# Pairing the leftover choices: a five-way branch near the end of a two-layer mixture kernel

## The chip, the cores and the metric

The kernel runs on one core of a Trainium2 chip. The metric is device time in microseconds (us) of that core, the median of several runs. A core has TensorE (PE in the profile; its weight loads are shown as PEld), VectorE (DVE), ScalarE (ACT), GpSimd (POOL) and SyncE (SP), each with an instruction stream of its own; the streams meet at semaphores.

## The reference, cut to what matters

Sixteen batches of 256 rows of 256 numbers pass through two residual layers. Layer 0 picks one expert of eight per batch (the largest entry of that batch's row of `cond_8`); layer 1 picks the two largest, weights them, and adds an expert that all batches share.

```python
# layer 0, per batch: expert = argmax(cond_8[b]); hidden size 512
out = (silu(x @ wu.T + bu) * (x @ wg.T + bg)) @ wd.T + bd
x = x + out
# layer 1, per batch: the two largest of softmax(cond_8[b]), weights w normed; hidden size 1024
out = sum(w[k] * ((gelu(x @ g[sel[k]]) * (x @ u[sel[k]])) @ d[sel[k]]) for k in range(2))
x = x + out + (gelu(x @ gs) * (x @ us)) @ ds       # the shared expert, for every batch
```

All is float32. Layer 1 thus has 32 routed choices (16 batches times two) and 16 shared ones. Which experts they fall on is known only when the kernel runs.

## The kernel before

**Units.** Work comes in units. A `Single` is one batch with one expert. A `Pair` is two batches that use the same expert; it multiplies both with Strassen's seven products in place of eight (`STEPS`), in Winograd's form. Its sums of weight blocks are made on POOL (`sums_a`, lines 353 to 357), those of x and of the hidden values on VectorE (`sums_b`, 346 to 349). A unit of layer 1 is cut into four quarters of the hidden size (two in layer 0). A single's quarter is 8 "up" matmuls (line 546, `p` and `pl`) and 4 "down" matmuls (line 575, `po`); a pair's is 14 up matmuls (line 407, banks X, Y, Q) and 7 down matmuls (line 458, `dX`, `dY`, `dQ`). All are 128 x 128 by 128 x 256.

**Order.** A routing computation on VectorE (`choices`, `order_of_work`) sorts the choices of each layer so that batches with the same expert stand side by side, and those without a partner at the end. 32 choices over 8 experts leave at most 8 experts with an odd number, so at least 12 pairs exist whatever the inputs: `NP2 = (NA - E) // 2` is 12. The last 8 positions (`NS2`) may or may not have partners. The kernel runs them all as singles. The sequence of units is fixed when the kernel is built:

```python
units = [*l0_pairs, *shared[:NF], *pairs, *ones[:-1], *shared[NF:]]
```

that is: 4 pairs of layer 0 with singles of layer 0 among them, 3 shared pairs, the 12 routed pairs, 7 singles, 5 shared pairs; the eighth single (`lone`) runs its quarters inside those of the fourth shared pair. Expert and batch numbers are read at run time from the sorted lists into registers of SP and POOL (`held`, line 235), so loads and stores have computed addresses.

**Timing by hand.** The instructions stand in the order that a hand-written clock gives (`Line`): `main` runs an up step and advances the clock, `later` puts a step some ticks behind (a pair's seventh up step, its activation, its downs), `flush` emits what is due. At each quarter `ahead` issues what later quarters need: `load_q` five quarters ahead (a 512 KB weight quarter, line 284, on SP's queue), the pair's POOL sums and `load_x` three ahead, `sums_x` one ahead, and `load_d` (1 MB, line 296) in the unit's own first quarter (its second in a layer 0 pair). Results go out on POOL's queue (`send`, line 329, an accumulating store in layer 1). The last pair adds to what stands in `out`, which `load_z` reads back in that pair's second quarter (j == 1), and stores from SP and ScalarE (line 494).

**Buffers** come from rotating pools with a number of buffers per tag (6 weight quarters `q`, 5 sums `s`, 2 down weights `d`, 3 results `ys` and so on), and PSUM banks X, Y, Q (two each), A and B (one each) likewise.

## Time and profile before

| what | value |
|---|---|
| runs | 1067.0, 1067.0, 1065.17 us (median 1067.0) |
| the profiled execution | 1065.7 us, of which the span from first to last instruction is 1064.1 us |
| matmul records on TensorE | 4858 (two for each fp32 matmul of the program) |
| granted TensorE clock | 1.00 |
| DMA | 146.26 MB, mean 137 GB/s |
| weight quarters loaded in layer 1 | 112 of 512 KB |
| ScalarE | 30% busy |

How to read the page: its first part gives each engine's busy time, share and number of instructions; the second cuts the span into 40 slices, each digit a busy share in tenths; the fourth follows the chain of work that ended last back from the end, so that shares in it are shares of what sets the time; a group row reads line, engine, operation, output<-input, shape, count, then busy time and mean ns, then idle time before it and what ended that. In a stretch's row the numbers after its length are the busy times of PE, PEld, DVE, ACT and POOL with instruction counts, then the granted clock, the DMA share and GB/s. A timeline row is start, length, then the instructions merged into it; a record of 1.89 us can overlap the next, as matmuls are pipelined.

### The profile page before, as it was taken

The numbers are of one execution on the slowest core, as the hardware profiler recorded it, in microseconds if no ns is written. First come the engines' busy times: TensorE is split into PE (matmuls) and PEld (weight loads), VectorE is DVE, ScalarE is ACT, GpSimd is POOL, SyncE is SP. The second block draws the span as 40 slices with busy tenths as digits, with TensorE's granted clock in tenths as the row PEclk, the third lists the DMA queues.
The fourth block names the chain that finished last, engine by engine and source line by source line (L and its number), as shares of the span: only waits on it lengthen the run. The fifth ranks groups of instructions, "written<-read, shape, count | busy, mean of one in ns | idle before, by whom it ended". The sixth has DMA issues, their size and how long they took to land.

```text
span 1064.1 us, 14030 instructions
## 1 busy us (share of the span) xinstructions
PE 1055.8 (99%) x4858; PEld 921.7 (87%) x4858; DVE 681.1 (64%) x1070; ACT 323.6 (30%) x516; POOL 472.7 (44%) x570
## 2 busy tenths in 40 slices
PE   9999999999999999999999999999999999999998
PEld 6788888888888888888888888888888888888887
DVE  7888775677767776777677777741111136767774
ACT  2222233333333333333333333321111122333331
POOL 2554454745663565466456535200000245554530
PEclk9999999999999999999999999999999999999999
DMA  7555565543453355235524542454656653453232
GB/s 254 188 198 195 182 206 169 177 131 91 117 139 99 99 133 140 88 96 139 139 99 100 139 129 85 114 148 127 171 198 178 183 183 119 129 139 102 61 76 40
DMA packets 50231, 146.26 MB, mean 137 GB/s; under 512 B 5234, under 2 KB 16114, under 8 KB 46578
## 3 DMA queue, kind: packets, MB, share of 16 engines
q1 hardware_dynamic: 35826, 124.66, 35.0%
q0 software_dynamic: 14048, 20.45, 11.2%
q8 instruction: 39, 0.64, 0.2%
q10 hardware_dynamic: 288, 0.26, 0.1%
q14 instruction: 30, 0.25, 0.1%
HBM read 124.38 MB, written 20.97 MB: 137 GB/s over the span
## 4 chain that ended last, share of the span: by engine, by line
PE 97%; DVE 1%; DMA 1%; issue 0%; SPq 0%; ACT 0%; DVEq 0%
PE X L407 21%; PE Y L407 14%; PE Q L407 14%; PE dX L458 11%; PE po L575 7%; PE p L546 7%; PE pl L546 7%; PE dQ L458 7%; PE dY L458 7%; DMA x<-x_dram 1%; PE spin L96 1%; DVE sq_z L159 0%; SPq L235 0%; ACT L433 0%; SPq L284 0%
## 5 line engine op out<-in xcount | busy, mean ns | idle before, releaser
L390 ACT ACTIVATE u<-X 128x512 f32<-128x512 f32 x264 | 157.6, 597 | 466.3 <-PE X L407 466.1
L354 POOL TENSOR_TENSOR s<-q 128x256 f32<-128x256 f32 x88 | 76.2, 865 | 252.5 <-PE Q L407 185.2
L407 PE MATMUL Y<-x,q 128*128 128x256 f32 x704 | 181.5, 380 | 2.4 <-DVE act L565 2.4
L407 PE MATMUL Q<-x,s 128*128 128x256 f32 x704 | 180.7, 379 | 0.0
L434 DVE TENSOR_TENSOR bt<-c 128x1024 f32<-128x1024 f32 x80 | 113.1, 1413 | 102.7 <-ACT c L433 102.7
L407 PE MATMUL X<-x,s 128*128 128x256 f32 x672 | 173.0, 380 | 0.0
L329 POOL DMA_DIRECT2D out_dram<-ys x46 | 47.5, 1032 | 255.3 <-ACT ys L587 108.5
L407 PEld LDWEIGHTS Y<-x,q 128*128 128x128 f32 x704 | 132.8, 190 | 22.8 <-DVE act L565 2.8
L407 PEld LDWEIGHTS Q<-x,s 128*128 128x128 f32 x704 | 133.8, 190 | 18.2
L407 PEld LDWEIGHTS X<-x,s 128*128 128x128 f32 x672 | 127.1, 190 | 19.1 <-issue 2.1
L394 DVE TENSOR_TENSOR c<-u,Q 128x512 f32<-128x512 f32 x176 | 119.8, 680 | 27.8 <-ACT u L390 23.4
L394 DVE TENSOR_TENSOR c<-u,Y 128x512 f32<-128x512 f32 x176 | 119.5, 679 | 11.7 <-PE Y L407 11.7
L557 DVE TENSOR_TENSOR act<-gel,pl 128x512 f32<-128x512 f32 x32 | 22.0, 686 | 124.7 <-PE pl L546 124.7
L575 PE MATMUL po<-act,d 128*128 128x256 f32 x384 | 89.8, 380 | 0.8 <-DVE act L565 0.7
L407 PE MATMUL X<-x,q 128*128 128x256 f32 x352 | 90.3, 379 | 0.0
L546 PE MATMUL pl<-x,q 128*128 128x256 f32 x368 | 86.9, 379 | 0.0
L546 PE MATMUL p<-x,q 128*128 128x256 f32 x368 | 86.9, 379 | 0.0
L433 ACT ACTIVATE c<-c 128x1024 f32<-128x1024 f32 x80 | 84.2, 1052 | 8.3 <-DVE c L394 7.6
L458 PE MATMUL dX<-bt,ds 128*128 128x256 f32 x352 | 83.9, 379 | 0.0
L458 PE MATMUL dQ<-bt,ds 128*128 128x256 f32 x352 | 83.8, 379 | 0.0
L458 PE MATMUL dY<-bt,d 128*128 128x256 f32 x352 | 83.8, 379 | 0.0
L575 PEld LDWEIGHTS po<-act,d 128*128 128x128 f32 x384 | 72.8, 190 | 11.4 <-DVE act L565 1.1
(117 smaller groups left out, 1324.2 us busy)
## 6 DMA issues: line engine op xcount, KB each, us to landing
q<-wq_dram SPq DMA_DIRECT2D x112, 512.0 KB, 3.5
d<-wd_dram SPq DMA_DIRECT2D x28, 1024.0 KB, 6.5
out_dram<-ys POOLq DMA_DIRECT2D x54, 256.0 KB, 4.4
x<-x1d SPq DMA_DIRECT2D x48, 256.0 KB, 4.1
q<-wq_dram SPq DMA_DIRECT2D x22, 514.0 KB, 4.0
d<-wd_dram SPq DMA_DIRECT2D x12, 513.0 KB, 5.4
x<-x_dram SPq DMA_DIRECT2D x15, 256.0 KB, 4.3
x1d<-ys POOLq DMA_DIRECT2D x8, 256.0 KB, 2.6
```

What stands on the lines that cost most here:

```text
L96: nc.tensor.matmul(spin, lhsT=idle[:, :P], rhs=idle, start=True, stop=True)
L329: nc.gpsimd.dma_start(row(out), ys[:, :, t, :], accum_op=ALU.add)
L354: tt(s("S1"), a("A21"), a("A22"), ALU.add)
L390: nc.scalar.activation(t, self.banks["X", j], AF.Copy)
L394: nc.vector.tensor_tensor(self.c[j][:, block].rearrange("p m s -> p (m s)"), self.copies[n, j], self.banks[tag, j], op,)
L407: nc.tensor.matmul(self.banks[tag, j][:, bass.ts(m, S)], lhsT=self.q[j][:, m, A_AT[a], :] if a in A_AT else self.s[j][:, m, S_AT[a], :], r ...
L433: nc.scalar.activation(u, u, AF.Gelu_apprx_tanh)
L434: nc.vector.tensor_tensor(t[:, 0:4, :], u, v, ALU.mult)
L458: nc.tensor.matmul(d, lhsT=src[:, j, :], rhs=self.acts[j][:, B_AT[b], :], start=OPENS[k] and j == 0, stop=j == self.kp - 1, skip_group_che ...
L546: nc.tensor.matmul(dst[:, bass.ts(half, S)], lhsT=self.q[j][:, m, 2 * half + c, :], rhs=self.xt[:, c, :], start=(c == 0), stop=(c == KD - 1),)
L557: nc.vector.tensor_tensor(act, gel, pu[1], ALU.mult)
L575: nc.tensor.matmul(self.po[:, bass.ts(c, S)], lhsT=self.d[:, 2 * c + half, j, :], rhs=self.acts[j][:, bass.ts(half, S)], start=(j == 0 and ...
```

## The change

Three things are changed.

1. **A count.** `order_of_work` for layer 1 already marks the last choice of each expert with an odd number (with 4096, in `count`). Now their sum is turned into `more`, the number of further pairs among the last 8 positions: 4 minus half the number of marks, as an integer `more_i` in SBUF.
2. **A branch.** All units up to the fifth shared pair and the first quarter lists of the sixth (`shared[-3]`) are emitted in common. Then every engine loads `more_i` into a register and jumps into one of five arms. Arm k runs the sixth shared pair, the 8 - 2k choices left as singles, k more pairs, and the last two shared pairs. Each arm is written out in full from the same saved state. There is no `lone` single any more. The weight load that would run five quarters ahead across the branch is the first load in the arm. `load_z` moves to the last pair's third quarter (j == 2). Three shared pairs run ahead of the 12 routed ones as before, but only two, not none, stand between these and the first single, besides the sixth in the arm.
3. **Fixed tiles.** The pools are replaced by lists of tiles of the same numbers and sizes (`RINGS`, `BANKS`), handed out in turn (`take`); for five tags a tile is returned by name (`give`), and steps that need one wait in the emission order until one is free (`when_free`).

The core of the diff:

```diff
+            yield red(more, count, AX.X, ALU.add)
+            nc.vector.tensor_scalar(more, more, -1.0 / (2 * 4096), NS2 / 2, ALU.mult, ALU.add)
+            yield nc.vector.tensor_scalar(more_i, more, 0.0, float(NS2 // 2), ALU.max, ALU.min)
...
+    def take(tag, *shape, of=None):
+
+        i = turns[tag].pop(0)
+        if tag not in HELD:
+            turns[tag].append(i)
+        else:
+            assert (tag, of) not in turns
+            turns[tag, of] = i
+        t = rings[tag][i]
...
+    def when_free(tag, f):
+
+        if turns[tag] and not turns["later", tag]:
+            f()
+        else:
+            turns["later", tag].append(f)
+
+    def give(tag, of):
+        turns[tag].append(turns.pop((tag, of)))
+        if turns["later", tag]:
+            turns["later", tag].pop(0)()
...
-            t = wp.tile([P, QB], F32, tag="q", name=f"q_{self.n}_{j}", bufs=6)
+            t = take("q", QB)
...
+    more_pairs = [Pair(next(names), 1, 2 * NP2 + 2 * i) for i in range(NS2 // 2)]
     ones = [Single(next(names), 1, 2 * NP2 + i) for i in range(NS2)]
-    lone = ones[-1]
-    units = [*l0_pairs, *shared[:NF], *pairs, *ones[:-1], *shared[NF:]]
-    units[-1].last = True
+    units = [*l0_pairs, *shared[:NF], *pairs, *shared[NF : NPR - NB]]
+    shared[-1].last = True
...
-            if u is units[-1] and j == 1:
+            if u is shared[-1] and j == 2:
                 u.load_z()
...
+    quarters += in_order(shared[-NB:-NB + 1])
+    run(units)
+    for _ in routing:
+        pass
...
+    common, entry = len(quarters), state()
+    which = nc.values_load(
+        more_i[0:1, 0:1],
+        min_val=0,
+        max_val=NS2 // 2,
+        skip_runtime_bounds_check_because="held between 0 and the largest when it is made",
+    )
+    for k in tc.Switch(which, NS2 // 2 + 1):
+        for o, d in entry:
+            o.clear()
+            o.update({n: v.copy() if isinstance(v, (list, dict)) else v for n, v in d.items()})
+        left = ones[2 * k :]
+        rest = [shared[-NB], *left, *more_pairs[:k], *shared[1 - NB :]]
+        quarters[common:] = in_order(rest)[shared[-NB].kp :]
+        u, j = quarters[common]
+        u.load_q(j)
+        run(rest)
+        line.flush(1 << 30)
+        line.send()
```

`NB` is 3 and `NS2` is 8.

## The prediction

> **What bounds the kernel now.** First the page's totals, the slices and the chain.

> ```profile
> span 1064.1 us, 14030 instructions
> ...
> PE 1055.8 (99%) x4858; PEld 921.7 (87%) x4858; DVE 681.1 (64%) x1070; ACT 323.6 (30%) x516; POOL 472.7 (44%) x570
> ...
> PE   9999999999999999999999999999999999999998
> ...
> PE 97%; DVE 1%; DMA 1%; issue 0%; SPq 0%; ACT 0%; DVEq 0%
> ```

> TensorE is busy in every slice and 97% of the chain is its own. So the time is the number of matmuls times the slot of one, plus the few places where TensorE stands still. The table by stretches for 330 to 696 us (pairs) and 696 to 878 us (mostly singles) says how few:

> ```profile
> 330.00:696.00 366.00, 365.96 (x1694) 320.64 (x1693) 267.23 (x388) 130.29 (x204) 188.07 (x206) 1.00 0.42 115
> 696.00:878.00 182.00, 182.00 (x845) 160.03 (x843) 39.72 (x60) 30.68 (x50) 27.87 (x31) 1.00 0.58 174
> ```

> The second column after the stretch is TensorE: no idle time in either, although VectorE (fifth number) works 73% of the pair stretch and 22% of the other. Asking for the waits of TensorE from 200 us to 1060 us gives none. A pair is therefore not held up by its extra sums, and a single not by its loads. The slot comes from the chain in order of time, in the stage of singles:

> ```profile
> 756.32 1.73 PE po L575 x8
> 758.05 1.73 PE p L546 x8
> 759.78 1.73 PE pl L546 x8
> ...
> 777.04 1.73 PE po L575 x8
> ```

> Each row holds 8 records, that is 4 matmuls of the program (an fp32 matmul leaves two records: 2,429 in the program, 4,858 on the page). Four quarters, one whole single, take 777.04 - 756.32 = 20.72 us for 48 matmuls: 0.4317 us each. A layer 1 pair has 84 matmuls (4 quarters of 7 x 2 up, 7 x 4 down), so 36.26 us; in the pair stretch the chain's piece "dX" at 237.34 recurs at 273.60 and 309.86, 36.26 us apart.

> **How far TensorE's sequencer runs ahead** decides what a branch costs. The built program has a semaphore wait of TensorE just ahead of each pair's first X matmul; the view of line 407 between 548.80 and 548.95 shows one, the timeline the matmuls after it:

> ```profile
> L407 PEldq EVENT_SEMAPHORE  x1: 51/51/51, 548.9 to 548.9; - x1
> ```

> ```profile
> 551.00 1.89 PE L458 MATMUL dY<-bt,d 128*128 128x256 f32 x8
> 552.73 1.03 PE L407 MATMUL X<-x,q 128*128 128x256 f32 x4
> ```

> The wait was over at 548.9 us, the matmul behind it began at 552.73: at the end of a pair the sequencer stands 3.8 us ahead of the array, and the same number recurs at each pair's end. The new branch is put in exactly such a place (Y, then four dY matmuls, then the next pair's X).

> [...]

> ```profile
> q8 instruction: 39, 0.64, 0.2%
> ```

> 39 packets of 16 KB[...]. [...]

> **The change, part by part.**

> *Which arm runs.* The two largest of each row of cond_8 as drawn by the reference choose experts 0 to 7 for 6, 2, 6, 3, 4, 4, 2, 5 batches. Halved and rounded down: 15 pairs, two choices left. Twelve are sure, so three more are paired: the fourth arm runs (three pairs, two singles).

> *Matmuls.* Three pairs replace six singles: 3 x (2 x 48 - 84) = 36 fewer of 2,429 (the built program agrees: 1,759 before the branch and 634 in that arm). 36 x 0.4317 = **15.5 us off the path**.

> *Loads.* Six singles load 24 q and 6 d, three pairs 12 and 3: 15 SP loads less, 9.4 MB. Nothing waited for them, so no gain.

> *Sums added.* 60 POOL operations at 0.865 us (the row of line 354), some 52 us, and about 21 us of VectorE per pair (26.5 for a pair, 267.2/366.0 of 36.26, less eight products of 0.686 from the row of line 557). Hidden: the 330 to 696 us stretch carries just this density of pairs with 0.04 us of TensorE idle. POOL sums start three quarters (27 us of pairs, 15 us of singles) ahead and need 3.5 us. If that cover went, TensorE would stand for the missing part of 3.5 us at each of 12 quarters.

> *Fixed tiles.* In the built program every engine's instructions keep their order up to the stage of singles, apart from three tiny VectorE operations for the count; TensorE has slightly fewer waits, POOL more (each some 20 to 50 ns while POOL idles 56%). The tile orders name the same readers. Cost 0. The z load is issued one quarter later and a store, its POOL queue and SP wait for it; z has more than 20 us until the last pair's downs. Cost 0.

> *The branch.* On each of five engines: a register load, two register steps, an indirect branch, the fetch of the arm's first block. The first register load of SP took 466 ns, of POOL 492 ns:

> ```profile
> L235 SPq TENSOR_LOAD <-bs x64: 262/272/517, 13.7 to 1010.1; - x64
> ```

> Take 0.5 us, 0.4 us for moves and branch, and for the fetch 2.4 us: 0.9 us for a 16 KB packet (0.2% of 16 x 1064 us over 39) and 1.5 us of latency, an estimate from the 128 KB stores that land in 1.8 us. Sum 3.3 us; bounds 2 and 7 us, as no row shows such a fetch.
> On **TensorE** this starts 3.8 us ahead of the array: 0 exposed at 3.3 us, 3.2 us at 7. **ScalarE** reaches its branch when the last pair's third X step ends, six matmuls (2.6 us) before TensorE's branch point, and must copy the first new X two matmuls (0.9 us) after it; TensorE's wait for that copy ends 0.9 us ahead of need in an earlier pair (by line 407's view the wait began at 552.9 and took 1512 ns, the X matmul behind it started at 555.32). Cover 2.6 + 0.9 + 0.9, some 4.2 us with the latency of a semaphore. Behind it in its queue stand the copies that free X; TensorE waits for them. **VectorE** ends its last sums 2 us after the branch point, and the first result that TensorE needs (a Y bank used again) is due 8 us after. **POOL and SP** reach the branch 16 and 20 us before TensorE (waits on earlier matmuls), and then wait anyway. So a fetch is covered on every engine up to a total of about 3.8 us; I take 0.7 us for refilling the queue and a fetch somewhat over cover, from 0 to 5 us. Not below zero: a branch saves no work.

> *Sum.* Against the profiled execution, 1065.7 us (span 1064.1 and 1.6 around it): 1065.7 - 15.5 + 0.7 = 1050.9. The median of the runs, 1067.0, lies 1.3 above it and gives 1052.2. I take **1051.5 us**. A difference of 0.2% (2.1 us) is what can be told from none.

> **Rivals.**
> 1. *The branch is exposed*: fetch 5 to 10 us, five engines fetching at once beside 16 busy queues[...]. For: no cold fetch is in the trace. Against: packets of 0.9 us. 2 to 7 us back: 1053.5 to 1058.5.
> 2. *Slower*: after the jump the streaming doesn't resume, and every block of the arm is fetched cold on TensorE. The arm holds 634 x 4 instructions and its waits, ten blocks; from 1.55 us exposed per block the gain is gone, at 3 us the time is 1065.7 - 15.5 + 30 = 1080. Against: 39 blocks were fetched in before with no TensorE wait.
> 3. *It doesn't do what it says*: a count of zero selects the first arm, 2,429 matmuls as before, 1067 us. The counts above speak against it.

> **How the numbers follow.** Forecast (0 to 2 us exposed, 1050 to 1053.5): 0.70. Rival 1: 0.20. Slower: 0.05. No change: 0.02. A little better than the sum: 0.03. The range runs from 1049.5, the full 15.5 off the fastest run, to 1057, within rival 1, leaving under 2 in 10 out. Faster 0.93, same 0.02, slower 0.05.

> **What would show it.** TensorE's count falls by 72 records to 4,786; its busy time by about 15.5 us. Around the branch (1,759 matmuls in, about 770 us) a gap on TensorE under 2 us. Of the eight singles of 20.7 us two are left, beside three more pairs of 36.3 us. POOL busy rises by some 50 us with no TensorE wait behind it. A gap of many us at the branch, or gaps every 27 us after it (a block's length), would make the prediction wrong, as would a count of records unchanged.

## The result and the profile after

The changed kernel takes **1071.9 us** (median of 5 runs, 1071.5 to 1074.22) against 1067.0 us before (1065.17 to 1067.46): a ratio of 1.0053, with a 95% interval of 1.0038 to 1.0067. It is slower by 4.9 us; 1051.5 us was forecast. All runs here have inputs that select the fourth arm; no other arm was timed. The profiled execution took 1071.5 us, of which the span is 1069.9 us. Its page, in the lines that answer to those shown of before:

```profile
span 1069.9 us, 14169 instructions
...
PE 1049.1 (98%) x4786; PEld 910.0 (85%) x4786; DVE 772.9 (72%) x1166; ACT 342.2 (32%) x546; POOL 573.8 (54%) x630
...
PE   8999999999999999999999999999979999999998
...
PE 85%; DVE 9%; issue 3%; ACT 2%; DMA 1%; SPq 0%; DVEq 0%; ACTq 0%
```

The work did fall: 4786 matmul records in place of 4858. But TensorE's busy time fell by 6.7 us only (1055.8 to 1049.1), and 9% of the chain is now VectorE's, 1% before. One digit of TensorE's row is a 7: the slice at 776 to 802 us, just behind the branch. The table by stretches, with the columns as before (after the stretch come its length, then TensorE, its weight loads, VectorE, ScalarE and POOL, each with a count in brackets; the granted clock is the third number from the end):

```profile
770.00:800.00 30.00, 23.39 (x93) 19.20 (x92) 16.58 (x21) 7.62 (x13) 8.48 (x6) 0.89 0.42 99
800.00:830.00 30.00, 30.00 (x141) 26.41 (x140) 17.08 (x28) 8.77 (x14) 1.08 (x1) 1.00 0.43 121
...
860.00:890.00 30.00, 30.00 (x139) 25.50 (x137) 10.09 (x16) 7.07 (x12) 18.66 (x22) 1.00 0.67 179
890.00:920.00 30.00, 26.85 (x113) 21.93 (x113) 24.68 (x34) 10.52 (x16) 18.71 (x21) 0.94 0.36 121
```

A full stretch of 30 us holds about 139 to 141 records. 770 to 800 us holds 93 and 890 to 920 us holds 113: fewer than the idle time explains (6.6 and 3.2 us), since in both the granted clock is below 1. TensorE's waits from 200 us on, of which there were none before (in total, times, longest):

```profile
PE Q L466 <- DVE c L451: 7.4, 4, 4.2
PE Y L466 <- DVE c L451: 1.8, 3, 1.4
PE X L466 <- issue: 0.9, 1, 0.9
PE A L518 <- DVE bt L494: 0.4, 1, 0.4
```

Apart from the branch's own "issue" they are all waits for VectorE, and nearly all for `c` of line 451, the sums that empty a bank so that a Y or Q matmul may use it again.

**Where the time went.** For each execution I set the start of every matmul record, in order, against an even slot of 0.2158 us (half of the 0.4317 us of a matmul), counted from the tenth record. What a record is late by this clock, in us:

| record | before | after |
|---|---|---|
| 3460 (758 and 761 us), the last pairs ahead of the branch | 13.8 | 16.8 |
| 3610, behind the branch | 13.8 | 27.1 |
| 3910, in the singles | 13.8 | 27.1 |
| 4160, in the pair that follows the singles | 13.9 | 33.7 |
| the last pairs (4780 of both) | 14.2 | 35.1 |

So after loses 3.0 us ahead of the branch (1.1 of it by record 500, in the first 120 us, the rest over the pairs behind that), **10.3 us at the branch**, **6.5 us in the first pair after the singles** (6.6, of which before has 0.1 too), and 1.1 us later: 20.9 us. From the profiled execution of before: 1065.7 - 15.5 + 20.9 = 1071.1, and 0.5 us more behind the last matmul, where the engines also branch out of the arm, make 1071.6; 1071.5 was measured. The saving is all there, and three new delays outweigh it.

**The branch.** Line 856 of the changed kernel is the load of `more_i` into a register, the view of it by engine (shortest, median, longest in ns, then first and last start in us):

```profile
L856 SPq TENSOR_LOAD <-more_i x1: 275/275/275, 753.7 to 753.7; - x1
L856 POOLq TENSOR_LOAD <-more_i x1: 293/293/293, 759.1 to 759.1; - x1
L856 PEldq TENSOR_LOAD <-more_i x1: 491/491/491, 769.9 to 769.9; - x1
L856 ACTq TENSOR_LOAD <-more_i x1: 470/470/470, 771.5 to 771.5; - x1
L856 DVEq TENSOR_LOAD <-more_i x1: 543/543/543, 775.5 to 775.5; - x1
```

Behind it come the moves, the branch, and the arm's first instruction. From the records of each sequencer (us):

| engine | branch begins | first instruction of the arm | between |
|---|---|---|---|
| SP | 754.2 | 757.6 | 3.4 |
| POOL | 759.6 | 762.15 | 2.5 |
| TensorE | 770.8 | 774.7 | 3.9 |
| ScalarE | 772.2 | 774.7 | 2.5 |
| VectorE | 776.7 | 784.2 | **7.5** |

The timeline of TensorE in after, from the branch on:

```profile
772.06 1.89 PE L518 MATMUL Y<-bt,d 128*128 128x256 f32 x8
774.88 1.10 PE L466 MATMUL X<-xt,q 128*128 128x256 f32 x4 [0.94 <-issue]
...
782.73 1.03 PE L466 MATMUL X<-xt,q 128*128 128x256 f32 x4
785.19 1.13 PE L466 MATMUL Y<-xt,q 128*128 128x256 f32 x4 [1.43 <-DVE c L451]
790.56 2.04 PE L466 MATMUL Q<-xt,s 128*128 128x256 f32 x4 [4.24 <-DVE c L451]
```

and that of VectorE:

```profile
775.50 0.43 DVE L406 TENSOR_TENSOR bt<-bt 128x256 f32<-128x256 f32 x1
784.45 0.69 DVE L451 TENSOR_TENSOR c<-cp,Y 128x512 f32<-128x512 f32 x1 [8.52 <-PE X L466]
785.05 0.68 DVE L451 TENSOR_TENSOR c<-cp,Q 128x512 f32<-128x512 f32 x1
...
786.86 2.96 DVE L494 TENSOR_TENSOR bt<-c 128x1024 f32<-128x1024 f32 x1 [0.80 <-ACT c L493]
```

TensorE's own branch costs 0.94 us of the array: its sequencer ran 4.0 us ahead (the load began at 769.9, and without the stop of 0.94 us the matmul behind the branch, at 774.88, would have been due at 773.94). VectorE's sequencer has no such lead: its load begins at 775.5, as its last sum of the pair does. Then VectorE stands for 8.52 us. (The releaser "PE X" in that row is only the last semaphore before the sum; the X it names had long ended, and it is the branch that ended last.) TensorE stops twice for it, and at 790.56 the four records of Q take 2.04 us in place of 1.03: after the stop of 4.24 us TensorE runs some 14 slots at half rate. From 790.56 to the next block at full rate, at 797.04, 16 records take 6.48 us instead of 3.45. So 0.94 + 1.43 + 4.24 + 3.0 = 9.6 of the 10.3 us, 8.7 of them behind VectorE.

### The profile page after: what moved, and what is told of

The parts are those of the page before. It is cut to its first block, busy times and chain, and to the rows that moved or that the text cites. A ratio compares the mean times of both kernels' runs of the same rounds, so it can differ in the third digit from the quotient of the medians.

```text
span 1069.9 us, 14169 instructions
## 1 busy us (share of the span) xinstructions
PE 1049.1 (98%) x4786; PEld 910.0 (85%) x4786; DVE 772.9 (72%) x1166; ACT 342.2 (32%) x546; POOL 573.8 (54%) x630
## 4 chain that ended last, share of the span: by engine, by line
PE 85%; DVE 9%; issue 3%; ACT 2%; DMA 1%; SPq 0%; DVEq 0%; ACTq 0%
PE X L466 21%; PE Q L466 14%; PE Y L466 14%; PE A L518 11%; PE B L518 8%; PE Y L518 7%; PE Y L643 3%; DVE c L451 3%; PE X L613 3%; PE Q L613 2%; DVE bt L404 1%; DVE bt L494 1%; ACT c L493 1%; PE Y L613 1%; DVE bt L405 1%
## 5 line engine op out<-in xcount | busy, mean ns | idle before, releaser
L447 ACT ACTIVATE cp<-X 128x512 f32<-128x512 f32 x300 | 178.7, 596 | 524.1 <-PE X L466 522.6
L466 PE MATMUL Q<-xt,s 128*128 128x256 f32 x736 | 191.2, 383 | 7.4 <-DVE c L451 7.4
L466 PE MATMUL Y<-xt,q 128*128 128x256 f32 x736 | 190.4, 381 | 2.0 <-DVE c L451 1.8
L466 PE MATMUL X<-xt,s 128*128 128x256 f32 x736 | 191.1, 382 | 0.0
L466 PEld LDWEIGHTS Q<-xt,s 128*128 128x128 f32 x736 | 140.4, 192 | 28.6 <-issue 6.8
L466 PEld LDWEIGHTS Y<-xt,q 128*128 128x128 f32 x736 | 138.5, 190 | 25.6 <-DVE c L451 7.0
L466 PEld LDWEIGHTS X<-xt,s 128*128 128x128 f32 x736 | 140.5, 192 | 21.2 <-issue 1.3
L451 DVE TENSOR_TENSOR c<-cp,Q 128x512 f32<-128x512 f32 x200 | 135.8, 679 | 26.2 <-ACT cp L447 21.3
L384 POOL DMA_DIRECT2D out_dram<-ys x46 | 49.0, 1066 | 184.9 <-DVE ys L551 68.8
L451 DVE TENSOR_TENSOR c<-cp,Y 128x512 f32<-128x512 f32 x200 | 135.6, 678 | 16.6 <-PE X L466 8.5
L414 POOL TENSOR_TENSOR s<-s,q 128x256 f32<-128x256 f32 x100 | 77.4, 774 | 113.0 <-PE Q L466 113.0
L412 POOL TENSOR_TENSOR s<-s,q 128x256 f32<-128x256 f32 x100 | 98.7, 987 | 8.4 <-PE Y L643 0.7
L518 PEld LDWEIGHTS Y<-bt,d 128*128 128x128 f32 x400 | 76.0, 190 | 10.3
```

The lines of the kernel that those rows point to most:

```text
L412: tt(s("S2"), s("S1"), a("A11"), ALU.subtract)
L414: tt(s("nS4"), s("S2"), a("A12"), ALU.subtract)
L447: nc.scalar.activation(t, self.banks["X", j], AF.Copy)
L451: nc.vector.tensor_tensor(self.c[j][:, block].rearrange("p m s -> p (m s)"), self.copies[n, j], self.banks[tag, j], op,)
L466: nc.tensor.matmul(self.banks[tag, j][:, bass.ts(m, S)], lhsT=self.q[j][:, m, A_AT[a], :] if a in A_AT else self.s[j][:, m, S_AT[a], :], r ...
L518: nc.tensor.matmul(d, lhsT=src[:, j, :], rhs=self.acts[j][:, B_AT[b], :], start=OPENS[k] and j == 0, stop=j == self.kp - 1, skip_group_che ...
```

## The experiments

My theory after these readings: three separate causes, (1) VectorE's fetch at the branch, (2) the fixed tiles, through the time at which POOL's sums start, (3) the place of the added pairs behind singles. The rivals: the added sums load VectorE and POOL too much wherever they stand (then neither branch nor tiles matter), and for the branch, TensorE's own fetch. All edits are to the changed kernel unless said otherwise; ratios are to the kernel before, with a 95% interval.

### The branch

**static3**: no branch, the fourth arm alone, three pairs and two singles fixed at build.

```diff
-    which = nc.values_load(
-        more_i[0:1, 0:1],
...
-    for k in tc.Switch(which, NS2 // 2 + 1):
+    for k in (3,):
```

> The changed kernel with the branch taken out: the fourth arm's units are emitted in line, the count isn't read. Theory A (the branch itself costs the 10.3 us between matmul records 3460 and 3610 of the changed kernel, since VectorE comes back from it 8.7 us after it began to read the count): 1071.9 - 10.3 = 1061.6 us, the stop near 890 us stays, at about 7 us. Theory B (the added sums load VectorE and POOL so much that stops come anyway, the branch only marks the place): 1068 to 1072 us, with the stop moved.

Measured: 1062.39 us, 0.9967 (0.9946 to 0.9988). The branch thus costs 9.5 us of the 20.9, and the rest stays with it gone. (The five runs lie between 1060.74 and 1065.74 us, so the half microsecond is not certain.)

**hint**: all five arms stay, but the count is read one pair earlier, and each engine then gets an instruction that prefetches the arm that the register selects.

```diff
-    run(units)
+    run(units[:-1])
...
+    which = nc.values_load(
+        more_i[0:1, 0:1],
...
+    tc.switch_hint(
+        {e: which for e in (E5.PE, E5.DVE, E5.Activation, E5.Pool, E5.SP)}, NS2 // 2 + 1, "more"
+    )
+    run(units[-1:])
...
-    for k in tc.Switch(which, NS2 // 2 + 1):
+    for k in tc.Switch(which, NS2 // 2 + 1, hint="more"):
```

> The changed kernel with the count read one pair (36 us) earlier on every engine, and a prefetch hint for the chosen arm placed there. Theory A with the block's fetch as the price: VectorE's branch falls from 8.7 us to about 1 us, the time to 1061 to 1063 us. If the price is in the branch and not in the fetch, or the hinted block is thrown out again before the branch: 1071 to 1073 us.

Measured: 1061.87 us, 0.9953 (0.9934 to 0.9971), the same as without a branch. The time from VectorE's branch to its arm is now 0.6 us, TensorE's 0.4; ScalarE, POOL and SP take 2.5, 2.5 and 3.5 us as before, which harms nothing.

**hint_dve** and **hint_others** split this by engine: the count is read early in both, but only VectorE prefetches in the one, and all but VectorE in the other. Against hint, first hint_dve, then hint_others:

```diff
-        {e: which for e in (E5.PE, E5.DVE, E5.Activation, E5.Pool, E5.SP)}, NS2 // 2 + 1, "more"
+        {e: which for e in (E5.DVE,)}, NS2 // 2 + 1, "more"
```

```diff
-        {e: which for e in (E5.PE, E5.DVE, E5.Activation, E5.Pool, E5.SP)}, NS2 // 2 + 1, "more"
+        {e: which for e in (E5.PE, E5.Activation, E5.Pool, E5.SP)}, NS2 // 2 + 1, "more"
```

> The count is read one pair early on all engines, but only VectorE prefetches its arm. If VectorE's fetch alone is what the branch costs, the time is that with all five prefetching, 1061.9 us, within 1 us, although TensorE's own branch takes some 3.8 us again (covered by its queue). If TensorE's fetch shares in the cost, 1063 to 1068 us.

> The count is read one pair early on all engines, and all but VectorE prefetch their arm. If VectorE's fetch alone is what the branch costs, only its register load (8.7 us of stop less 1.2 us) is gone: 1069.5 to 1071.5 us. If TensorE's fetch shares in the cost, or if four fewer fetches at the jump make VectorE's quick, 1063 to 1067 us.

Measured: hint_dve 1062.06 us, 0.9949 (0.9934 to 0.9964); hint_others 1071.78 us, 1.0049 (1.003 to 1.0068). VectorE's timeline in hint_others, at the branch:

```profile
783.87 0.69 DVE L451 TENSOR_TENSOR c<-cp,Y 128x512 f32<-128x512 f32 x1 [8.53 <-issue]
```

and in hint_dve:

```profile
775.43 0.42 DVE L406 TENSOR_TENSOR bt<-bt 128x256 f32<-128x256 f32 x1
776.44 0.69 DVE L451 TENSOR_TENSOR c<-cp,Y 128x512 f32<-128x512 f32 x1 [0.58 <-PE Y L466]
```

The stop is 8.53 us without VectorE's prefetch, as in after, although the count was in its register long before (so the register load was not what was waited for; I had expected 1.2 us from taking it away), and gone with it. The fetch of VectorE alone is the branch's cost; the four other engines' fetches cost nothing measurable. The rival of TensorE's fetch is out.

**small_d** asks why VectorE's fetch takes 7.5 us and ScalarE's 2.5. In the records of the transfers, the 8 KB packets of an instruction fetch follow 0.9 us behind ScalarE's branch, but 4.6 us behind VectorE's (at 781.35 and 781.75). The records do not say which engine a packet is for; I assign them by time. One at 777.67 I take for a later one of ScalarE's, as hint_others has such a packet (774.97) ahead of VectorE's branch (775.52). The sixth shared pair's 1 MB load of down weights, issued at 773.98 and landed 7.4 us later, lies between, and VectorE's packets come as it ends (781.4). In hint_others they come as it ends too (780.75 and 781.16; landed at 781.1), though VectorE's branch began 1.2 us earlier there, which is why the early register load brought nothing.

```diff
-            nc.sync.dma_start(t[:, : src.shape[1]], src)
+            n = 128 if self is shared[-NB] else src.shape[1]
+            nc.sync.dma_start(t[:, :n], src[:, :n])
```

> The changed kernel with the down weights of the sixth shared pair loaded to a sixteenth only (the other columns of that tile stay what they were, so that pair's results are not the reference's). Its 1 MB load is under way when VectorE asks for its arm's first instructions. If that transfer holds up the instruction fetch: VectorE's branch falls from 7.5 us to about 2.5 us as on ScalarE and POOL, and the time to about 1064 us. If VectorE's branch is slow by itself: 7 to 8 us again, and 1071 to 1073 us.

Measured: 1068.29 us, 1.001 (1.0002 to 1.0019). VectorE's time in the branch falls to 4.3 us (777.77 to 782.07). So the load is worth 3.2 of the 7.5 us, and 3.6 us of the time (at the branch itself 5.9: record 3610 falls back by 4.4 us, not 10.3). Why the remaining 4.3 us is still above the 2.5 of ScalarE is not settled. In small_d's records VectorE has two packets, which end 2.6 us behind its branch, and ScalarE one, which ends 1.35 us behind; from there to the first instruction it is 1.7 and 1.2 us.

### The fixed tiles

**pools15**: the kernel *before* with 15 pairs fixed at build, one single ahead of the fourth shared pair and the other (`lone`) inside it. **pools15_order**: the same with the order of the changed kernel and no `lone`. The first edit is in both, the second in pools15_order (which also drops the loop that put `lone` into the pair, and has `load_z` at j == 2).

```diff
-NP2 = (NA - E) // 2
+NP2 = (NA - 2) // 2
```

```diff
-    lone = ones[-1]
-    units = [*l0_pairs, *shared[:NF], *pairs, *ones[:-1], *shared[NF:]]
+    lone = None
+    units = [*l0_pairs, *shared[:NF], *pairs[:12], *shared[NF:6], *ones, *pairs[12:], *shared[6:]]
```

> The kernel before with 15 routed pairs in place of 12, fixed when built, so one single and the one inside the fourth shared pair are left: no branch, no count, rotating pools. Theory A (36 matmuls less are worth their 15.5 us where nothing else is changed): 1067.0 - 15.5 = 1051.5 us. Theory B (VectorE and POOL cannot carry the three further pairs): 1058 us or more, with waits of TensorE for VectorE in the last third.

> As the kernel before with 15 routed pairs fixed when built and rotating pools, but in the changed kernel's order: 12 pairs, three shared pairs, two singles, three pairs, two shared pairs, no single inside a shared pair. If the stop near 890 us comes from this order (a pair straight after singles, its sums late): 1058 to 1059 us. If it comes from the fixed tiles: 1051.5 to 1053 us.

Measured: 1054.28 us, 0.9889 (0.9868 to 0.991), and 1058.35 us, 0.9921 (0.9904 to 0.9937). The three added pairs do save what the prediction says: pools15 lies 2.8 us above 1051.5, and its only TensorE wait after 200 us is one of 2.7 us, on the other single's down weights:

```profile
PE po L575 <- DMA d<-wd_dram: 2.7, 1, 2.7
```

Against pools15_order, static3 differs by the fixed tiles (and the three small operations for the count and the place of one weight load): 1062.39 - 1058.35 = **4.0 us** in medians, with a spread of 5 us among the runs of static3. The matmul records give it more narrowly: from record 500 to 3460, the stage of pairs, static3 falls back by 4.3 us and pools15_order by 1.5, so **2.8 us** are lost in the pairs; another 1.5 us is there by record 500 already, where static3 ran at half rate once, at 33 us, and pools15_order did not (mean clocks 0.997 and 0.998). The profile says how the pairs lose. The timeline of POOL in before (pools), one quarter's four sums:

```profile
337.64 0.73 POOL L354 TENSOR_TENSOR s<-q 128x256 f32<-128x256 f32 x1 [6.58 <-PE Q L407]
338.46 0.73 POOL L355 TENSOR_TENSOR s<-s,q 128x256 f32<-128x256 f32 x1
339.14 0.73 POOL L356 TENSOR_TENSOR s<-q 128x256 f32<-128x256 f32 x1
339.84 0.72 POOL L357 TENSOR_TENSOR s<-s,q 128x256 f32<-128x256 f32 x1
```

and in after (fixed tiles):

```profile
333.17 0.73 POOL L411 TENSOR_TENSOR s<-q 128x256 f32<-128x256 f32 x1 [2.65 <-PE Q L466]
333.98 0.73 POOL L412 TENSOR_TENSOR s<-s,q 128x256 f32<-128x256 f32 x1
334.67 1.71 POOL L413 TENSOR_TENSOR s<-q 128x256 f32<-128x256 f32 x1
339.28 0.73 POOL L414 TENSOR_TENSOR s<-s,q 128x256 f32<-128x256 f32 x1 [2.90 <-PE Q L466]
```

In before the first sum into a buffer waits for the whole buffer (6.58 us, until the last matmul that reads it), and then four run in one go. In after each waits for the readers of its own block only: three start 4.5 us earlier, the fourth waits again. Earlier is worse here, as the third now falls on VectorE's product of line 494, which writes `bt` (334.08, 1.71 us; in before 332.51, 1.22 us), and others, by the two rows below, on the sums of `bt`. The rows of line 347 in before and of line 404 in after, the same sums (330 to 690 us):

```profile
L347 DVE TENSOR_TENSOR bt<-bt 128x512 f32<-128x512 f32 x40 | 33.7, 843 | 0.0
```

```profile
L404 DVE TENSOR_TENSOR bt<-bt 128x512 f32<-128x512 f32 x39 | 43.1, 1104 | 0.0
```

In two such meetings in after the later one takes longer: the POOL sum beside that product 1.71 us in place of 0.73, a VectorE sum of 0.42 us 1.37 (after, line 405 at 792.75, beside POOL's of 1.71 us at 792.13), and each of the two ends 0.14 us less than its own time behind the end of the other (0.59 and 0.28 us behind). The sums of line 451 do not show this: all take 0.67 to 0.69 us in after, the two at 789.74 and 790.34 beside POOL's of 2.14 us at 788.81 too. What the two engines share was not shown.

**static3_first** puts the pools' timing back: one write of two elements per partition to the fourth block, ahead of the sums. POOL then waits for that block first.

```diff
+            nc.gpsimd.memset(s[:, :, S_AT["nS4"], 0:1], 0.0)
             self.sums_a(lambda n: q[:, :, A_AT[n], :], lambda n: s[:, :, S_AT[n], :])
```

> The kernel static3 (no branch, fourth arm in line) with one added POOL write of 2 elements per partition to the last block of each quarter's sums, ahead of its four sums, so that all four start only when the last reader of the old sums is done, as with the rotating pools. If the fixed tiles cost about 4 us because the first three sums now start earlier and run beside VectorE's own sums: POOL's sums and VectorE's line 404 go back to about 0.73 to 0.90 us and 0.84 us each in the stage of pairs, and the time falls from 1062.4 to about 1058.5. If the 4 us come from other waits of the fixed tiles: 1062 to 1063 us.

Measured: 1059.34 us, 0.9928 (0.9914 to 0.9942); against static3 3.05 us off with 100 instructions added. VectorE's busy time falls from 772.7 to 747.5 us. Its row of line 404, 330 to 690 us:

```profile
L404 DVE TENSOR_TENSOR bt<-bt 128x512 f32<-128x512 f32 x40 | 32.9, 823 | 0.0
```

Record 3460 is late by 14.1 us, not 18.3, and 3.2 us of that difference arise behind record 500: from there to 3460 static3_first falls back by 1.1 us, static3 by 4.3. This is less than pools15_order's 1.5, so this one effect is all that the fixed tiles cost in the pairs.

**hint_first** is both mends in the changed kernel, with its five arms and its order.

> Both mends together in the order of the changed kernel: the count is read and the arm prefetched one pair early (1061.9 us alone), and POOL's four sums of a quarter start together (3.05 us in the kernel without a branch, 1062.39 to 1059.34). If the two causes are separate, they add: 1061.9 - 3.0 = 1058.9 us, within 1.0 us of it. If the gain of the earlier count came partly from the sums (they share VectorE), less: 1060.5 to 1062 us.

Measured: 1059.94 us, 0.9932 (0.9919 to 0.9946): 12.0 us below after. Of the second mend's 3.05 us 1.93 are left beside the first (hint was 1061.87). That is between the two forecasts, 0.04 us outside the first and 0.6 below the rival's, and the medians can't decide. The records do: from record 500 to 3460 hint falls back by 4.1 us and hint_first by 1.3, so the second mend brings 2.8 us there beside the first, against 3.2 alone.

### The pair that follows the singles

What remains in hint_first is one place, its record 4160 being 7.9 us later than its record 3910 by the even slot. TensorE's timeline there:

```profile
885.30 1.10 PE L467 MATMUL Q<-xt,s 128*128 128x256 f32 x4 [1.63 <-DVE c L452]
...
891.22 1.13 PE L467 MATMUL Y<-xt,q 128*128 128x256 f32 x4 [0.29 <-DVE c L452]
894.86 2.04 PE L467 MATMUL Q<-xt,s 128*128 128x256 f32 x4 [2.50 <-DVE c L452]
```

A pair's ups wait for VectorE to empty banks. In a row of pairs the 7 x 4 downs of the pair before stand among them, and a quarter takes 21 matmuls, 9.07 us. After singles there are no such downs: a quarter is 14 matmuls, 6.04 us, while VectorE's share of a pair, 26.5 us over four quarters by the pair stretch of before, is 6.6 us. The kernel before never met this: its `lone` single filled the fourth shared pair. pools15 keeps that and has no stop there (records 3910 and 4160 late by 18.0 both); pools15_order has it, late by 14.4 and 21.9.

**static3_mixed** (static3) and **mended** (both mends) spread the singles, so that no two stand together: single, pair, single, pair, pair. In both, a single's running sum and a pair's down product fall into one Y bank, so that a part of the sums of layer 1 is changed.

```diff
-        rest = [shared[-NB], *left, *more_pairs[:k], *shared[1 - NB :]]
+        rest = [shared[-NB]]
+        for i in range(k + 1):
+            share = -(-len(left) // (k + 1 - i)) if k < 3 else 1
+            rest += left[:share] + more_pairs[i : min(i + 1, k)]
+            left = left[share:]
+        rest += shared[1 - NB :]
```

> The kernel static3 with the two singles put apart: single, pair, single, pair, pair. A pair straight after one single still has downs of the pair before it among its first ups. If the stop of 4 to 7 us near 890 us comes from a pair that runs without such downs (14 matmuls or 6.0 us per quarter against some 6.6 us of VectorE work): the stop goes, 1062.4 - 5 = 1056 to 1058 us. If it comes from POOL catching up after any single: two such stops, 1062 to 1066 us.

> The changed kernel with all three mended and all five arms kept: hint a pair ahead, POOL's sums started together, singles put between pairs. If the three causes are right and add up: 1061.9 - 4 - 5, about 1053 us; the full gain would be 1051.5. If one of the three was misread: 1057 to 1062 us.

Measured: 1062.21 us, 0.9955 (0.994 to 0.9969), and 1061.02 us, 0.9944 (0.9932 to 0.9957). Both missed: nothing gained. The stop only moved, to the second pair that follows a single; mended's timeline of TensorE:

```profile
920.92 1.10 PE L467 MATMUL Q<-xt,s 128*128 128x256 f32 x4 [0.92 <-DVE c L452]
927.69 1.13 PE L467 MATMUL Y<-xt,q 128*128 128x256 f32 x4 [1.14 <-DVE c L452]
931.33 2.05 PE L467 MATMUL Q<-xt,s 128*128 128x256 f32 x4 [2.50 <-DVE c L452]
```

So the missing downs alone do not explain the stop, and the question became what makes VectorE late: POOL's sums beside it, or its own work.

**small_sums**: hint_first, with POOL's sums for the first added pair cut short.

```diff
+            w = 8 if self is more_pairs[0] else P
-            self.sums_a(lambda n: q[:, :, A_AT[n], :], lambda n: s[:, :, S_AT[n], :])
+            self.sums_a(lambda n: q[:, :, A_AT[n], :w], lambda n: s[:, :, S_AT[n], :w])
```

(and `sums_d` likewise)

> The kernel with both mends (prefetched arm, POOL's sums starting together; 1059.94 us), but for the first of the three added pairs, the one that follows the singles, POOL's sums of weights cover 8 of 128 columns; the rest of the summed blocks keeps old values, so that pair's results are not the reference's. TensorE, ScalarE and VectorE do the same instructions. If that pair's stop (TensorE 4.4 us idle in 860 to 920 us, and slots at half clock behind it) comes from POOL's sums slowing VectorE's beside them, it goes: 1054 to 1056 us. If VectorE's own work of 6.6 us a quarter against 6.04 us of matmuls is enough for it, the stop stays: 1058.5 to 1060 us.

Measured: 1059.9 us, 0.9939 (0.9925 to 0.9953), but its profiled execution, the fastest of five, took 1057.17 us. TensorE's waits in it from 700 us on:

```profile
PE Q L469 <- DVE c L454: 2.7, 2, 2.5
PE A L521 <- DVE bt L497: 0.4, 1, 0.4
PE Y L469 <- DVE c L454: 0.3, 1, 0.3
```

Neither theory alone. The first stop, of 1.63 us, is gone, so it was POOL's; the second, of 2.50 us, stands as it was. Behind it the profiled execution has no half-rate slots (mean clock 1.000), the other four, of 1059.15 to 1060.37 us, have a mean clock of 0.994 to 0.997: half-rate slots would account for the gain that they lack, though only their mean clock is known (the half rate is taken up in the next section). What VectorE does ahead of the second stop, in hint_first:

```profile
887.63 1.21 DVE L404 TENSOR_TENSOR xt<-xt 128x512 f32<-128x512 f32 x1
888.87 0.83 DVE L405 TENSOR_TENSOR xt<-xt 128x256 f32<-128x256 f32 x1
889.74 0.83 DVE L406 TENSOR_TENSOR xt<-xt 128x256 f32<-128x256 f32 x1
```

These are the next pair's x sums, 2.9 us in the fourth quarter of a pair that is already late. Its first quarter has VectorE idle for 2.8 and 4.3 us.

**x_early**: hint_first, with the x of the second pair behind the singles summed three quarters earlier (and loaded four earlier). **x_early_small**: the same with the short POOL sums.

```diff
...
-                if u.width == 2 and j == 0:
+                if u.width == 2 and j == 0 and u is not self.early:
                     u.sums_x()
+            if i + 7 in at and at[i + 7] == (self.early, 0):
+                self.early.load_x()
+            if i + 4 in at and at[i + 4] == (self.early, 0):
+                self.early.sums_x()
...
+        line.early = rest[len(left) + 2] if left else None
```

> The kernel with both mends (1059.94 us), but the second of the added pairs has its x loaded and summed three quarters earlier: in the first quarter of the pair ahead of it, where VectorE idles some 12 us. If the second stop (2.5 us at 892 us in that kernel) comes from these 2.9 us of sums standing in a quarter in which VectorE is already late, it goes with its half-clock slots, and the first (1.63 us) stays or shrinks: 1056 to 1057.5 us. If VectorE is short in these quarters wherever the sums stand, the stop only moves: 1059 to 1060.5 us.

> As x_early, and for the first added pair POOL's sums of weights cover 8 of 128 columns (the rest keeps old values, so that pair's results are not the reference's). If the two stops have these two causes, both are gone: TensorE without idle time from 860 to 900 us and 1053.5 to 1055.5 us. If VectorE's own work is too much, 1057 to 1059.5 us.

Measured: x_early 1056.44 us, 0.9902 (0.9888 to 0.9916); x_early_small 1054.92 us, 0.9887 (0.9872 to 0.9902). TensorE's waits from 700 us on, of x_early:

```profile
PE Q L467 <- DVE c L452: 2.0, 3, 1.6
PE A L519 <- DVE bt L495: 0.4, 1, 0.4
```

and of x_early_small:

```profile
PE A L521 <- DVE bt L497: 0.4, 1, 0.4
PE Q L469 <- DVE c L454: 0.3, 2, 0.2
```

The second stop goes when three operations of VectorE move to a quarter where it has time, the first when POOL's sums are short: two causes. Moving the x sums brings 3.5 us, and the short POOL sums, which are a test and leave out most of the sums, 1.5 us on top. By the records 3910 to 4160, the pair behind the singles costs 7.9 us in hint_first, 3.8 in x_early and 2.2 in x_early_small. Mended fits this: its pair without a stop is followed by a single, so no x sums stand in that pair's fourth quarter; in the pair that stops they begin at 924.09, ahead of the stops that end at 927.69 and 931.33. **x_early beats both kernels**: 10.4 us below before and 15.5 below after, with all five arms kept.

## Why the prediction was wrong

It was wrong in the sign: 1051.5 us forecast, 5% given to slower.

*Which arm runs, and the matmuls*: right. 4786 records; pools15 shows the gain of 15.5 us to within 2.8 us, and x_early_small, whose remaining waits are 0.7 us, to within 3.4.

*Loads, z*: right, no TensorE wait in after names a load. In pools15 alone a load of down weights shows, 2.7 us.

*The branch*: **the step that failed** is "VectorE ends its last sums 2 us after the branch point, and the first result that TensorE needs (a Y bank used again) is due 8 us after", and from it "a fetch is covered on every engine up to a total of about 3.8 us; I take 0.7 us". The two places are about right: the last sum ends 1.05 us after the matmul behind the branch (775.93 and 774.88), and TensorE could have run that Y at 783.76, 8.9 us after. Two things were wrong with them.
- The size. The fetch was taken at 2.4 us on every engine, 7 us the bound of the sum. It was 2.5 on ScalarE and POOL, 3.4 on SP, 3.9 on TensorE, but 7.5 us on VectorE, and with load and moves 8.7 us. The branch instruction itself is short: its record in after takes 0.04 to 0.06 us on four engines (on TensorE, where it spans the fetch, 3.8); the 0.4 us for moves and branch in the prediction's sum was an estimate. No part of this runs ahead of VectorE's work, as it does on TensorE.
- The kind of cover. "Due 8 us after" is the slack of one result, not time that VectorE has to spare. By the pair stretch of before it works 73% of the time, so a stop of 8.5 us puts some 6 us of sums off (an estimate, 0.73 x 8.5), and the next results are each due in turn. The first came 1.43 us late, the next 4.24 us, and with 3.0 us of slots at half rate that makes 8.7 us.

TensorE's part was right: the sequencer's lead (3.8 us forecast, 4.0 us seen) covered a branch of 4.75 us, from the start of the load to the arm's first instruction, but for 0.94 us. Of the rivals, the first named the right mechanism ("fetch 5 to 10 us") and priced it at 2 to 7 us; it took 9.5. Its reason of five engines fetching at once did not hold (with four of the fetches moved away, in hint_others, VectorE stops for 8.53 us as before); that of busy queues did in part (small_d). The second rival did not happen: TensorE's waits after the branch name VectorE only. (Its ten blocks are an estimate: 634 of 2,429 matmuls, times the 39 packets of before.)

On the half rate: behind the stop of 4.24 us in after, slots take near 0.43 us in place of 0.216. But the length of a stop does not decide alone. One of 2.50 us has half-rate slots behind it in hint_first (the next two rows of four records take 2.04 and 1.81 us) and none in the profiled execution of small_sums (1.10 and 1.03 us); one of 2.00 us has them in after (the Q at 898.47, 1.59 us, and the X behind it, 1.91), one of 2.38 us has none in before (a Y at 33.19, 1.13 us).

The traces of before and after show what parts the last two. In after the granted clock is 0.5 from 789.71 to 796.54 us and from 898.94 to 902.35, and again from 1069.61, behind all matmuls; these dates lie 2, 32, 33 and 82 times 3.413 us behind the first. In before it changes once, at 1063.40, also behind all matmuls. Cut each trace into stretches of 3.413 us at these dates and add up TensorE's idle time in each that ran at full rate. The four with 2.00 us idle or more were followed by half rate (after: 3.39 us from 786.30, 2.00 from 895.53, all of the one from 1066.19, behind the last matmul; before: 2.81 from 1059.99, at the end), none of those with 1.77 us or less was. In before the stop of 2.38 us is cut by a date at 32.57 us and leaves 1.77 in one stretch. So in these two traces the place of a stop counts beside its length; that this also parts hint_first from small_sums was not shown. By the mean clock the executions of one kernel fall into groups: all those of before that were run beside the experiments and had a mean clock of 0.999 or 1.000 took 1064.84 to 1066.69 us, those with 0.998 or less 1066.62 to 1069.64 us. A half-rate stretch of 3.41 us costs up to 1.7 us, half its length (an estimate), so differences of that size between single executions say little.

*Fixed tiles*: **failed**. "The tile orders name the same readers. Cost 0." They name the same readers, but per block instead of per buffer, so POOL's sums start earlier. It cost 4.0 us in medians (static3 against pools15_order) and 2.8 us by the records of the pairs; one small write gave back 3.05 and 3.2. The step argued from the order of instructions on each engine, which says nothing about when a wait ends.

*Sums added*: **failed**. "Hidden: the 330 to 696 us stretch carries just this density of pairs with 0.04 us of TensorE idle." That stretch has pairs behind pairs, with 9.07 us a quarter; the added pairs begin behind singles, with 6.04 us a quarter against 6.6 us of VectorE. It cost 6.5 us by the records (after, 3910 to 4160). The prediction's bound ("TensorE would stand for the missing part of 3.5 us") looked at POOL's sums coming late; none did. What came late was VectorE, and POOL only slowed it.

*The sum*: forecast 1051.5; then, in medians of runs, the order of pairs behind singles and what comes with it, 1058.35 (pools15_order); fixed tiles, 1062.39 (static3); branch, 1071.9.

Not settled: why VectorE's fetch needs 4.3 us even without the large load; what the last 1 us between static3_first (1059.34) and pools15_order (1058.35) comes from (in their profiled executions 0.5 us is there by record 500 and 0.7 arise behind record 4160, none in the pairs between); what the 2.2 us are that x_early_small still loses in the pair behind the singles, with waits of only 0.7 us; and whether a single inside a pair would mend the order with fixed tiles as it does with pools, which was not tried.

## What to carry to other kernels

Price a branch for each engine by itself: here the engine whose sequencer did not run ahead of its work paid the whole fetch, and its cover was the idle time that it had, not the date of its next result; a prefetch of the target one pair earlier brought 10 us back. A stretch that shows an engine's load to be hidden shows it for that neighbourhood only: before moving work, compare each engine's time in a step with the time of the matmuls of that very step. Finer dependencies let work start earlier, and where two engines lengthen each other's operations (0.42 us to 1.37, 0.73 to 1.71), earlier can be the wrong time.
